# Layer 0's back part: pairs of chunks, or one chunk in each of five parts

## Chip, cores and metric

The kernel runs on one core of one Trainium2 chip. The metric is device microseconds (us) of one execution of the whole program; the median of several executions is given, and one execution is recorded by the hardware profiler.

## What is computed

Two layers on an image of 64 x 64 pixels with 96 channels. Each layer adds a state-space mixer to the image and then a small MLP whose operands are rounded to fp8. Only the end of layer 0's mixer, layer 0's MLP and the first projection of layer 1 matter here:

```
y = _layernorm(y1 + y2 + back(y3) + back(y4), ln_g, ln_b)   # 192 channels
x = x + (y * silu(z)) @ out_proj_w                           # 192 -> 96
t = _ln_t(x)                                                 # per pixel, 96 channels
h = relu(q_acc(q_acc(q_mul(t) @ q_mul(W1).T) + q_mul(b1)))   # 96 -> 384
x = x + q_acc(q_acc(q_mul(h) @ q_mul(W2).T) + q_mul(b2))     # 384 -> 96
xz = _ln_c(x) @ W_in.T                                       # layer 1: 96 -> 192 used here
```

## The kernel before

The 4096 pixels are eight chunks of 512. `back0` (L1019) runs the lines above once for each chunk. The short names used below are those of the tiles:

- **m** (`centred`, L1064): the mean over 192 channels, as 512-column fp32 matmuls with a constant matrix, for a pair of chunks at once, because the upper 64 channels of two chunks share one tile; VectorE subtracts it (L1075, L1076), ScalarE squares (**sq**, L1079), GpSimd multiplies by the gate (L1081).
- **ov** (`variance`, L1083): the variance of the pair by three matmuls (L1088), its root on ScalarE (osd, L1090), a transfer into another layout on the SP queue (or, L1093), a reciprocal on VectorE (L1094).
- **o** (`gated_out`, L1098): the output projection of a chunk, eight matmuls of 128x96 (L596, L597) in one PSUM tile; VectorE scales each quarter by the factor and adds it to the image (L1106). Then `mlp_norm` (L1957): `norm_chunk` (L159: two sums and two scalings on VectorE, a square and a root on ScalarE), rounded to fp8, copied to bf16 by GpSimd (**xb**, L1960).
- **tf** (`mlp_turn`, L1963): four transposes of xb, copied to **xf** by ScalarE (L189).
- **h** (`mlp_up`, L1969): three 512-column matmuls h0, h1, h2 (L1977) from xf, each into one of two PSUM buffers. ScalarE casts each to fp16 (L1979); the bias and relu of h0 run on ScalarE (L1981), those of h1 and h2 on VectorE (L1983); GpSimd casts to fp8 (h8, L1985).
- **of** (`mlp_down`, L1988): twelve matmuls of 128x96 (L1997) that take the three h8 tiles in turn, four times; ScalarE casts (L2002), VectorE adds bias and image (L2003, L2004). Then `norm_chunk` again, giving **lnxnc**.
- **tr** (`to_layer1`, L1109): four fp32 transposes of lnxnc, copied to xt by ScalarE (L189) and stored (L1114).
- **in** (`keep_in_proj`, L1117; `in_proj`, L327): two 512-column fp32 matmuls into layer 1's padded image, copied by ScalarE and VectorE (L333).

The order on TensorE is written out by hand: every matmul goes through `keep` (L1061), which holds it in program order. The order on VectorE, ScalarE and GpSimd is chosen by a scheduler when the program is built; each engine then runs its list in order. PSUM buffers: three for m and in, two shared by ov, o and of, two for h, one shared by tf and tr.

The loop of `back0` goes over four pairs of chunks. For a pair, TensorE's order is m (of this pair, in the step before), o of both chunks, tr and in of the previous pair's two chunks, ov of the next pair, tf of both, h of both, of of both. Layer 1's convolution follows the last in; its first matmul is L1176, then L1209.

Of the kernel before, what the change touches and what calls it, by code (L numbers as in the profile page):

```python
# [28 lines left out]
F32 = mybir.dt.float32  # L29
# [5 lines left out]
ALU = mybir.AluOpType  # L35
# [4 lines left out]
P = 128  # L40
# [3 lines left out]
CD = 96  # L44
# [3 lines left out]
HID = 384  # L48
CH = 512
NCH = L // CH  # L50
# [56 lines left out]
def chunk(c):  # L107
    return slice(c * CH, (c + 1) * CH)
# [12 lines left out]
class Net:  # L121
# [897 lines left out]
    def back0(self):  # L1019

        tc = self.tc
        self.xn_d = self.scratch("xn1", [CD, L])
        with ExitStack() as ctx:
            self.tp = ctx.enter_context(tc.tile_pool(name="af0", bufs=3))
            self.lp = ctx.enter_context(tc.tile_pool(name="al0", bufs=2))
            self.pa = ctx.enter_context(tc.tile_pool(name="ps_a0", bufs=3, space=PSUM))  # L1030
            self.po = ctx.enter_context(tc.tile_pool(name="ps_o0", bufs=2, space=PSUM))
            self.ph = ctx.enter_context(tc.tile_pool(name="ps_h0", bufs=2, space=PSUM))
            self.pt = ctx.enter_context(tc.tile_pool(name="ps_t0", bufs=1, space=PSUM))
            self.w_in = self.w_in1
            n = NCH // 2
            self.sq, self.factor, self.xb, self.xn, self.xt, self.hid = {}, {}, {}, {}, {}, {}

            def chunks(s):
                c0 = s // 2 * 4 + s % 2
                return (c0, c0 + 2) if 0 <= s < n else ()  # L1040

            for s in range(-1, n + 1):
                if s + 1 < n:
                    self.centred(s + 1, chunks(s + 1))
                if 0 <= s < n:
                    self.gated_out(s, chunks(s))
                for c in chunks(s - 1):
                    self.to_layer1(c)
                for c in chunks(s - 1):
                    self.keep_in_proj(c)  # L1050
                if s + 1 < n:
                    self.variance(s + 1, chunks(s + 1))
                for c in chunks(s):
                    self.mlp_turn(0, c)
                for c in chunks(s):
                    self.mlp_up(0, c)
                for c in chunks(s):
                    self.mlp_down(0, c)
                    self.xn[c] = self.norm_chunk(self.lp, c, self.eps6, F32, f"c{c}")

    def keep(self, instruction):  # L1061
        self.tc.keep_in_program_order(instruction)
# [32 lines left out]
        for k, c in enumerate(chunks):  # L1095
            self.factor[c] = r[:, k]

    def gated_out(self, s, chunks):  # L1098

        nc = self.nc  # L1100
        for c in chunks:
            o = self.po.tile([P, 4, CD], F32, tag="o", name=f"o0{c}")
            self.out_proj(o, self.y, self.wg, c, self.keep)
            for j in range(4):
                to, r = self.res[:, c, j, :], self.factor[c][:, j : j + 1]
                nc.vector.scalar_tensor_tensor(to, o[:, j, :], r, to, ALU.mult, ALU.add)  # L1106
            self.mlp_norm(0, c)

    def to_layer1(self, c):  # L1109
        nc = self.nc  # L1110
        xt = self.tp.tile([CD, CH], F32, tag="xt1", name=f"xt1{c}")
        t = self.pt.tile([P, CH], F32, tag="t", name=f"tr1{c}")
        self.to_channels(t, self.xn.pop(c), self.ident, xt, keep=self.keep)
        nc.sync.dma_start(self.xn_d[:, chunk(c)], xt)  # L1114
        self.xt[c] = xt

    def keep_in_proj(self, c):  # L1117
        self.in_proj(self.pa, "a", self.xt.pop(c), self.pad1, c, f"1{c}", self.keep)

# [844 lines left out]
        self.to_channels(t, self.xb.pop(c), self.identb, xt, "c (j p) -> c j p", self.keep)  # L1966
        self.xt[c] = xt

    def mlp_up(self, li, c):  # L1969

        nc = self.nc
        w1, w2, b1, b2 = self.mlp_w[li]
        xt = self.xt.pop(c)
        self.hid[c] = []
        for m in range(HID // P):
            a = self.ph.tile([P, CH], F32, tag="h", name=f"h{li}{c}{m}")
            self.keep(nc.tensor.matmul(a, w1[:, m * P : (m + 1) * P], xt, start=True, stop=True))  # L1977
            h16 = self.tp.tile([P, CH], F16, tag="h16", name=f"h16{li}{c}{m}")
            nc.scalar.copy(h16, a)  # L1979
            if m == 0:  # L1980
                nc.scalar.activation(h16, h16, AF.Relu, bias=b1[:, m : m + 1])  # L1981
            else:
                nc.vector.tensor_scalar(h16, h16, b1[:, m : m + 1], 0.0, ALU.add, ALU.max)  # L1983
            h8 = self.tp.tile([P, CH], FP8, tag=f"h8{m}", name=f"h8{li}{c}{m}")
            nc.gpsimd.tensor_copy(h8, h16, saturate=False)  # L1985
            self.hid[c].append(h8)
# [100 lines left out]
```

## Time and profile before

| quantity | us |
|---|---|
| median of 11 runs (1486.65 to 1496.18) | 1487.85 |
| profiled execution | 1487.29 |
| its span, first to last instruction | 1485.5 |
| the back of layer 0: first m to layer 1's first matmul | 120.74 to 280.71 |
| TensorE busy from 119 to 281 | 128.19 |
| VectorE, ScalarE, GpSimd busy there | 75.32, 59.55, 35.27 |

How to read the views: the page divides the span into 40 slices and gives a digit for the busy tenths of each engine, and for the clock granted to TensorE. Busy time can be asked for any stretch of the span. The waits say which instruction of which engine ended the idle time of an engine, with total, number and longest. The timeline lists instructions with start and duration in us, and in brackets the idle time before. PE is TensorE, DVE VectorE, ACT ScalarE, POOL GpSimd, SP the queue of the transfers. A fp32 matmul shows as two records.

### The profile page before, as it was taken

The numbers are of one execution on the slowest core, as the hardware profiler recorded it, in microseconds if no ns is written. First come the engines' busy times: TensorE is split into PE (matmuls) and PEld (weight loads), VectorE is DVE, ScalarE is ACT, GpSimd is POOL, SyncE is SP. The second block draws the span as 40 slices with busy tenths as digits, with TensorE's granted clock in tenths as the row PEclk, the third lists the DMA queues.
The fourth block names the chain that finished last, engine by engine and source line by source line (L and its number), as shares of the span: only waits on it lengthen the run. The fifth ranks groups of instructions, "written<-read, shape, count | busy, mean of one in ns | idle before, by whom it ended". The sixth has DMA issues, their size and how long they took to land. (4 is left out here: it accounts for less than half of the span.)

```text
span 1485.5 us, 13012 instructions
## 1 busy us (share of the span) xinstructions
PE 1182.8 (80%) x4040; PEld 493.9 (33%) x4040; DVE 1155.5 (78%) x887; ACT 907.5 (61%) x1091; POOL 785.2 (53%) x461
## 2 busy tenths in 40 slices
PE   7998887799995477667777677687777888899875
PEld 4533444343331122222222222222222343344343
DVE  6593445203337999999999999999999999999875
ACT  4463333204446677677777777777777777787434
POOL 1002221100001787778777877777778777875545
PEclk9998666799997688888888888988888898987955
DMA  2242000013217745635555454645364557342201
GB/s 63 63 138 56 11 11 12 11 29 85 78 49 216 224 137 178 239 115 159 181 172 182 135 183 159 189 128 187 121 227 130 179 161 252 123 148 71 87 0 43
DMA packets 68851, 183.21 MB, mean 123 GB/s; under 512 B 21488, under 2 KB 35460, under 8 KB 61956
## 3 DMA queue, kind: packets, MB, share of 16 engines
q1 hardware_dynamic: 67480, 182.00, 39.8%
q8 instruction: 34, 0.56, 0.2%
q10 hardware_dynamic: 1292, 0.28, 0.1%
q14 instruction: 45, 0.37, 0.1%
HBM read 155.98 MB, written 20.47 MB: 119 GB/s over the span
## 5 line engine op out<-in xcount | busy, mean ns | idle before, releaser
L1552 POOL TENSOR_TENSOR hss<-h1s,xws 128x1024 f32<-128x1024 f32 x96 | 224.6, 2377 | 132.3 <-PE hs L1560 132.3
L1536 ACT ACTIVATE da<-dt1s,a 128x1024 f32<-128x1024 f32 x168 | 187.8, 1118 | 149.0 <-DVE xws L1547 87.8
L1560 PE MATMUL hs<-hss,ident 128*128 128x512 f32 x376 | 212.0, 647 | 58.9 <-DMA x2s<-bc 32.9
L1547 DVE TENSOR_TENSOR_SCAN xws<-da,xws 128x1024 f32<-128x1024 f32 x96 | 224.1, 2335 | 10.4 <-DVE xws L1547 2.7
L1536 ACT ACTIVATE da<-dt0s,a 128x1024 f32<-128x1024 f32 x168 | 187.0, 1113 | 69.3 <-DVE xws L1547 52.2
L1560 PE MATMUL hs<-h0s,ident 128*128 128x512 f32 x376 | 199.3, 612 | 0.4 <-DVE h0s L1547 0.4
L1547 DVE TENSOR_TENSOR_SCAN h1s<-da,h1s,xws 128x1024 f32<-128x1024 f32 x72 | 169.2, 2350 | 10.4 <-ACT da L1536 1.3
L1560 PEld LDWEIGHTS hs<-hss,ident 128*128 128x128 f32 x376 | 68.6, 200 | 193.2 <-issue 78.4
L1375 POOL TENSOR_TENSOR dun<-u,dtn 128x512 f32<-128x512 f32 x4 | 5.9, 1482 | 197.8 <-DVE dtn L1272 107.6
L1560 PEld LDWEIGHTS hs<-h0s,ident 128*128 128x128 f32 x376 | 74.2, 198 | 97.7 <-issue 92.5
L1581 PE MATMUL acc<-hc2s,fold 128*32 128x512 f32 x128 | 47.1, 825 | 61.0 <-POOL hc2s L1570 57.9
L1581 PE MATMUL acc<-hc0s,fold 128*32 128x512 f32 x128 | 46.3, 813 | 53.4 <-POOL hc0s L1570 53.4
L1581 PE MATMUL acc<-hc1s,fold 128*32 128x512 f32 x128 | 46.5, 816 | 50.1 <-POOL hc1s L1570 50.1
L1520 POOL TENSOR_TENSOR x1s<-x1s,dus 128x1024 f32<-128x1024 f32 x32 | 75.1, 2368 | 8.9 <-DMA x1s<-bc 8.9
L1520 POOL TENSOR_TENSOR x2s<-x2s,dus 128x1024 f32<-128x1024 f32 x32 | 75.1, 2362 | 6.6 <-DMA c1s<-bc 6.6
L1547 DVE TENSOR_TENSOR_SCAN x0s<-da,x0s 128x1024 f32<-128x1024 f32 x32 | 74.7, 2335 | 4.3 <-ACT da L1536 1.9
L1547 DVE TENSOR_TENSOR_SCAN x1s<-da,x1s 128x1024 f32<-128x1024 f32 x32 | 74.7, 2335 | 3.5 <-ACT da L1536 0.9
L1547 DVE TENSOR_TENSOR_SCAN x2s<-da,x2s 128x1024 f32<-128x1024 f32 x32 | 74.7, 2335 | 3.4 <-ACT da L1536 0.8
L1560 PE MATMUL hs<-x0s,ident 128*128 128x512 f32 x128 | 66.9, 604 | 0.2 <-DVE x0s L1547 0.2
L1560 PE MATMUL hs<-x1s,ident 128*128 128x512 f32 x128 | 66.6, 602 | 0.0
L1520 POOL TENSOR_TENSOR x0s<-x0s,dus 128x1024 f32<-128x1024 f32 x28 | 65.7, 2361 | 0.0
L1232 PE MATMUL cv<-pad,cw 128*128 128x512 f32 x144 | 64.3, 598 | 0.0
(343 smaller groups left out, 2415.8 us busy)
## 6 DMA issues: line engine op xcount, KB each, us to landing
c0s<-bc SPq DMA_DIRECT2D x184, 128.0 KB, 2.6
c1s<-bc SPq DMA_DIRECT2D x184, 128.0 KB, 2.6
x2s<-bc SPq DMA_DIRECT2D x32, 512.0 KB, 5.0
x0s<-bc SPq DMA_DIRECT2D x28, 512.0 KB, 3.5
x1s<-bc SPq DMA_DIRECT2D x28, 512.0 KB, 6.0
dus<-du SPq DMA_DIRECT2D x20, 512.0 KB, 7.0
dt1s<-dt SPq DMA_DIRECT2D x40, 256.0 KB, 6.5
dt0s<-dt SPq DMA_DIRECT2D x40, 256.0 KB, 4.8
```

The lines of the kernel that those rows point to most:

```text
L1232: keep(nc.tensor.matmul(t, cw[0][:, tap, 0:P], v, start=tap == 0, stop=False))
L1375: keep(nc.gpsimd.tensor_tensor(dun, u[1][:, m], dtn, ALU.mult))
L1520: keep(nc.gpsimd.tensor_tensor(x, x, du[:, part[j]], ALU.mult))
L1536: keep(nc.scalar.activation(das[i, s], dts[o][:, part[j]], AF.Exp, scale=self.a6[:, g, k : k + 1]))
L1547: keep(nc.vector.tensor_tensor_scan(to, da, x, start, ALU.mult, ALU.add))
L1552: keep(nc.gpsimd.tensor_tensor(cols(hs)[:, w, :], grid(h1)[:, w, :], grid(xw)[:, w, :], ALU.add))
L1560: keep(nc.tensor.matmul(t, self.ident, x[:, chunk(m)], start=x is hs, stop=x is xs[i % 3]))
L1581: keep(nc.tensor.matmul(to, self.fold4, src, start=k == 0, stop=k == NK - 1))
```

## The change

The loop goes over twelve steps. In step t, of goes to chunk t-3 of the sequence, in to chunk t-4, m or ov (in turn) to the pair t // 2, o to chunk t-1, tf and h to chunk t-2, and tr to chunk t-3, between the second and third h. The order inside a step is as written. `gated_out` takes one chunk, `mlp_up` takes the list of the blocks to do, the norms' pool has three buffers for each tile, and layer 1's turned chunks have their own dictionary.

```diff
-            self.lp = ctx.enter_context(tc.tile_pool(name="al0", bufs=2))
+            self.lp = ctx.enter_context(tc.tile_pool(name="al0", bufs=3))
...
             def chunks(s):
                 c0 = s // 2 * 4 + s % 2
-                return (c0, c0 + 2) if 0 <= s < n else ()
-
-            for s in range(-1, n + 1):
-                if s + 1 < n:
-                    self.centred(s + 1, chunks(s + 1))
-                if 0 <= s < n:
-                    self.gated_out(s, chunks(s))
-                for c in chunks(s - 1):
-                    self.to_layer1(c)
-                for c in chunks(s - 1):
-                    self.keep_in_proj(c)
-                if s + 1 < n:
-                    self.variance(s + 1, chunks(s + 1))
-                for c in chunks(s):
-                    self.mlp_turn(0, c)
-                for c in chunks(s):
-                    self.mlp_up(0, c)
-                for c in chunks(s):
-                    self.mlp_down(0, c)
-                    self.xn[c] = self.norm_chunk(self.lp, c, self.eps6, F32, f"c{c}")
+                return (c0, c0 + 2)
+
+            def chunk_of(q):
+                return chunks(q // 2)[q % 2] if 0 <= q < NCH else None
+
+            for t in range(NCH + 4):
+                s = t // 2
+                out, up, down, last = (chunk_of(t - d) for d in (1, 2, 3, 4))
+                if down is not None:
+                    self.mlp_down(0, down)
+                    self.xn[down] = self.norm_chunk(self.lp, down, self.eps6, F32, f"c{down}")
+                if last is not None:
+                    self.keep_in_proj(last)
+                if s < n:
+                    (self.variance if t % 2 else self.centred)(s, chunks(s))
+                if out is not None:
+                    self.gated_out(out)
+                if up is not None:
+                    self.mlp_turn(0, up)
+                    self.mlp_up(0, up, (0, 1))
+                if down is not None:
+                    self.to_layer1(down)
+                if up is not None:
+                    self.mlp_up(0, up, (2,))
...
-    def gated_out(self, s, chunks):
+    def gated_out(self, c):
...
-        for c in chunks:
-            o = self.po.tile([P, 4, CD], F32, tag="o", name=f"o0{c}")
-            self.out_proj(o, self.y, self.wg, c, self.keep)
-            for j in range(4):
-                to, r = self.res[:, c, j, :], self.factor[c][:, j : j + 1]
-                nc.vector.scalar_tensor_tensor(to, o[:, j, :], r, to, ALU.mult, ALU.add)
-            self.mlp_norm(0, c)
+        o = self.po.tile([P, 4, CD], F32, tag="o", name=f"o0{c}")
+        self.out_proj(o, self.y, self.wg, c, self.keep)
+        for j in range(4):
+            to, r = self.res[:, c, j, :], self.factor[c][:, j : j + 1]
+            nc.vector.scalar_tensor_tensor(to, o[:, j, :], r, to, ALU.mult, ALU.add)
+        self.mlp_norm(0, c)
...
-    def mlp_up(self, li, c):
+    def mlp_up(self, li, c, parts):
...
-        for m in range(HID // P):
+        for m in parts:
```

More of the change, by code (lines that the diff above doesn't have):

```diff
@@ L1035, in back0 @@
             n = NCH // 2
-            self.sq, self.factor, self.xb, self.xn, self.xt, self.hid = {}, {}, {}, {}, {}, {}
+            self.sq, self.factor, self.xb, self.xn, self.xt, self.xt1, self.hid = {}, {}, {}, {}, {}, {}, {}
             def chunks(s):
                 c0 = s // 2 * 4 + s % 2
-                return (c0, c0 + 2) if 0 <= s < n else ()
-            for s in range(-1, n + 1):
-                if s + 1 < n:
-                    self.centred(s + 1, chunks(s + 1))
-                if 0 <= s < n:
-                    self.gated_out(s, chunks(s))
-                for c in chunks(s - 1):
-                    self.to_layer1(c)
-                for c in chunks(s - 1):
-                    self.keep_in_proj(c)
-                if s + 1 < n:
-                    self.variance(s + 1, chunks(s + 1))
-                for c in chunks(s):
-                    self.mlp_turn(0, c)
-                for c in chunks(s):
-                    self.mlp_up(0, c)
-                for c in chunks(s):
-                    self.mlp_down(0, c)
-                    self.xn[c] = self.norm_chunk(self.lp, c, self.eps6, F32, f"c{c}")
+                return (c0, c0 + 2)
[20 more added lines that the diff above has]
+                    self.mlp_up(0, up, (2,))
     def keep(self, instruction):
@@ L1114, in to_layer1 @@
         nc.sync.dma_start(self.xn_d[:, chunk(c)], xt)
-        self.xt[c] = xt
+        self.xt1[c] = xt
     def keep_in_proj(self, c):
-        self.in_proj(self.pa, "a", self.xt.pop(c), self.pad1, c, f"1{c}", self.keep)
+        self.in_proj(self.pa, "a", self.xt1.pop(c), self.pad1, c, f"1{c}", self.keep)
     def layer1(self, w, pool):
@@ L1967, in mlp_turn @@
         self.xt[c] = xt
-    def mlp_up(self, li, c):
+    def mlp_up(self, li, c, parts):
         nc = self.nc
         w1, w2, b1, b2 = self.mlp_w[li]
-        xt = self.xt.pop(c)
-        self.hid[c] = []
-        for m in range(HID // P):
+        xt = self.xt[c]
+        self.hid.setdefault(c, [])
+        for m in parts:
             a = self.ph.tile([P, CH], F32, tag="h", name=f"h{li}{c}{m}")
```

## The prediction

> **What bounds the kernel now.** First the page. The changed code runs in slices 4 to 8 of 40 (37.1 us each), and there the tensor engine is the fullest engine, but it has gaps (the digits give the busy tenths of each slice):
>
> ```profile
> PE   7998887799995477667777677687777888899875
> ```
>
> The busy time by stretches cuts this out. Columns: length, busy time of PE, weight loads, DVE, ACT, POOL, then granted clock. The stretches are pair 1, pair 2, pair 3 without the next pair's mean, the drain, and the whole stage from its first matmul to layer 1's first.
>
> ```profile
> 160.50:198.40 37.90, 31.69 (x103) 17.07 (x101) 18.69 (x44) 14.12 (x28) 8.74 (x11) 0.68 0.04 11
> 198.40:236.40 38.00, 31.56 (x103) 17.09 (x101) 18.69 (x44) 14.12 (x28) 8.73 (x11) 0.68 0.04 11
> 236.40:267.00 30.60, 24.07 (x90) 15.06 (x88) 16.30 (x39) 11.76 (x24) 4.77 (x8) 0.61 0.06 14
> 267.00:281.00 14.00, 8.07 (x19) 3.79 (x18) 6.20 (x13) 4.46 (x9) 0.00 (x0) 0.59 0.10 28
> 119.00:281.00 162.00, 128.19 (x402) 68.15 (x402) 75.32 (x172) 59.55 (x114) 35.27 (x48) 0.67 0.09 23
> ```
>
> PE sets the pace; about 34 us of 162 are PE waits. Who ends them, from the waits of PE in this stage:
>
> ```profile
> PE tf L188 <- POOL xb L1960: 10.3, 5, 3.1
> PE tr L188 <- DVE lnxnc L180: 6.2, 2, 4.4
> PE of L1997 <- POOL h L1985: 5.6, 8, 0.7
> PE h L1977 <- ACT h L1979: 5.0, 8, 0.7
> ```
>
> The first two (16.5 us) are norm chains PE reaches too early. The last two (10.6) are the hidden layer's chain: PE h, ACT cast, DVE relu, POOL cast, PE of. In the timeline of pair 1 (start, length) its end reads:
>
> ```profile
> 190.46 0.42 PE L188 MATMUL tf<-identb,xb 128*96 128x128 bf16 x4 [2.55 <-POOL xb L1960]
> ...
> 195.39 0.58 ACT L1979 CAST h<-h 128x512 f16<-128x512 f32 x1
> ...
> 196.00 0.71 DVE L1983 TENSOR_SCALAR h<-h,b 128x512 f16<-128x512 f16 x1 [0.74 <-ACT h L1979]
> ...
> 196.84 0.81 POOL L1985 CAST h<-h 128x512 fp8e5<-128x512 f16 x1 [0.28 <-DVE h L1983]
> ...
> 197.70 0.98 PE L1997 MATMUL of<-w2q,h 128*128 128x96 fp8e5 x10 [0.74 <-POOL h L1985]
> ```
>
> From the end of the second tf (190.88) to the last relu'd block's use (197.70) are 6.8 us, paid once per **two** chunks. Last, the clock, in stretches I set to its own steps: the transitions lie 3.41 us apart or multiples of it.
>
> ```profile
> 135.11:138.52 3.41, 3.41 (x12) 2.94 (x11) 1.12 (x4) 1.12 (x2) 3.10 (x3) 1.00 0.00 0
> 138.52:141.93 3.41, 3.41 (x11) 2.60 (x10) 0.56 (x3) 0.00 (x0) 0.00 (x0) 0.50 0.01 2
> 145.35:148.76 3.41, 3.41 (x5) 0.31 (x3) 2.37 (x7) 0.70 (x2) 0.50 (x1) 0.50 0.00 0
> 148.76:152.17 3.41, 0.49 (x5) 0.28 (x4) 1.29 (x3) 1.86 (x4) 0.36 (x1) 1.00 0.04 1
> ```
>
> The output projection (128x96, all of 135.11 to 138.52) fills PE, yet the clock then halves; 512-column fp32 matmuls (m, ov, in) for about 2.9 us of a stretch or more bring it back, 1.85 us do not (159.0 to 162.4). I use this as the rule of this trace.
>
> **The change, part by part.** Nothing is removed or added in arithmetic: the same matmuls, evictions and eight `or` transfers. What moves is PE's hand-written order. A step now runs: of(c), in(c'), then m of a pair (even steps) or ov (odd steps), o(c''), tf, h0, h1, tr, h2 - and the next step opens with of of the very chunk whose h2 was just issued.
>
> Prices: fp32 512-column record 0.92 us at clock 0.50 and 0.44 at 1.00 (in: 8 records in 5.09 us from 251.59, 2.9 of it slow: 3.2 + 4.8 records). o of a chunk 5.1 to 5.7 (8 x 0.64 or 0.71). tf 0.4, tr 1.1, of's last ten matmuls 1.0.
>
> *Gone:* tf's wait (10.3): xb is now made a step earlier; its chain (o's end to tf about 5.1 us, 143.7 to 148.8) lies under the next step's of, in, m or ov and o (over 12 us); without that cover it costs 5.1 a step. h's wait (5.0) for its PSUM buffer: tr's 1.1 us stands there. Part of the drain: in of chunk 5 lies beside the last norm.
>
> *New 1: tf to h.* Between tf and h0 PE has nothing: ACT copies xf (0.58 and two hops), 0.75 us each step.
>
> *New 2: h2 to of.* Behind of stand in, m/ov and o, all of PE. The **tail** from tf's end to of's third matmul, on ACT's queue with the rows' lengths: odd step: xf to 0.69, cast h0 to 1.8, cast h1 to 2.35, relu h0 to 3.0, copy xt to 3.55, cast h2 to 4.1, then DVE 0.6, POOL 0.7 and hops: **5.75**. Even step: two squares of the pair (0.63 each) and lnsqb stand between: **6.65**. PE works 2.75 of each (three h, tr, two of), so it idles 3.0 or 3.9.
>
> *New 3: tr* needs lnxnc, made by DVE and ACT behind the in copies: hidden under o in steps 3 to 7. In step 8 (no m) DVE holds o's first eviction ahead of that norm's second sum, in step 9 (no o) ACT holds its square behind cast h0 and its root behind cast h1: tr starts 2.2 and 3.4 us after h1, and the tails are 7.7 and 8.8 (each piece again at its row's length).
>
> *Costed at nothing:* the third norm buffer (al0 2 to 3), DVE (75.3 busy of 162) and POOL (35.3); or's transfer (issue 188.30 to reciprocal 190.96, 2.7 us) lies under o (5.2 us), else it costs up to 2.7 an odd step. On SP one xn store per step stands ahead of the next or, its data ready before.
>
> Ledger, in us on the profile's clock (a step t counts from of's third matmul). A run of in with m or ov goes slowly until the first boundary (155.58, 159.0, 162.4 and so on) that ends a stretch it filled for 2.5 us or more. t4: 172.65 to 176.06 slow, 3.7 records, the other 8.3 at 0.44 take 3.65, in all 7.05. t6 starts 2.1 us ahead of a boundary and must go on to the next: 6 records slow in 5.5, 6 fast in 2.65.
> - t0 to t2: same to 130.0; o 135.6, m 138.7, o 144.2. tf waits for xb 5.1 us here, since ov no longer fills it: 149.7; tail without tr 5.4: 155.1 (of is already running, which the old order reached at 156.7).
> - t3: of 1.0 + ov 4.15 + o 5.25 + tf 0.4 + 5.75 = 16.55 to 171.65.
> - t4: 1.0 + in and m 7.05 + 5.3 + 0.4 + 6.65: 192.05. t5: 1.0 + in and ov 6.2 + 5.1 + 0.4 + 5.75: 210.5.
> - t6: 1.0 + 8.15 + 5.2 + 0.4 + 6.65: 231.9. t7: 1.0 + 6.8 + 5.1 + 0.4 + 5.75: 250.95.
> - t8: 1.0 + in 3.1 + o 5.2 + 0.4 + 7.7: 268.35. t9: 1.0 + in 3.7 + 0.4 + 8.8: 282.25.
> - drain: of 1.0, in 3.7, its copy 0.7 ahead of the norm on DVE, norm 3.1, tr 1.0, xt 0.75, in 3.65, copy 0.8: 296.95.
>
> Layer 1's first matmul was at 280.71: **+16.2 us**. So a pair t4+t5 is 38.85 against 37.9, t6+t7 40.45; the rest is fill and drain, where waits two chunks once shared are now paid by each. The profiled execution took 1487.29 (span 1485.5): 1503.5, I say 1503; the median 1487.85 differs by 0.6, which I leave.
>
> Bounds: tails are not in the old trace; below, PE's own work in one (2.75), above, the old two-chunk tail 6.8 and 2 us of misplaced queue. Dense runs: 9.2 us a pair at full clock, 19.3 at half; I take 13 to 15, nearest to the 13.4 of the old pair, as a run must cross one slow stretch.
>
> A rule on the clock speaks the other way. The Trainium skill ("TensorE: Matmul & The Clock Gate", section "Why this matters for your kernels") says that gaps under about 3 us keep the clock full. The trace differs: the clock halved at 138.5 after PE had been 3.41 of 3.41 us busy. By the rule all dense runs would be fast (17 us less, about 1486).
>
> **Rivals.**
> 1. *The tail is hidden, faster.* Were h8 ready when PE has issued h2, steps 3 to 9 lose 3.0+3.9+3.0+3.9+3.0+4.95+6.05 = 27.8 us: 1475.5. For it: waits of 16.5 us do go. Against: nothing stands between h2 and of on PE, and ACT's five pieces before cast h2 alone take 3 us. Deciding point: a mean wait ahead of of and h0 under 1.7 us a step rather than 4.0.
> 2. *A wash.* Tails 1 us shorter (7 us), and five dense runs meet a clock boundary one stretch sooner (1.78 each, 8.9): 1487.
> 3. *The clock stays half* through dense runs: 12 or 10 records at 0.92, some 14.5 us more: 1518. Against: a run of over 7 us always holds a whole slow stretch.
> 4. That one chunk per step is not what happens is excluded: PE's order is kept by hand, and it holds one chunk of each part per step.
>
> **How the numbers follow.** Forecast 0.81 (1492 to 1512), hidden tail 0.06, wash 0.07 (of it 0.02 faster), half clock 0.06. Within 0.2% is about what a measurement can tell from no change. Faster 0.08, same 0.05, slower 0.87. The range takes the forecast with tails 1 us off either way and clock boundaries one stretch off: 1491 to 1512.
>
> **What would show it.** Right: PE waits of "of <- POOL h" near 2 to 3 us each in steps 3 to 9 (some 20 in sum, from 5.6), h behind ACT xf near 0.75 eight times, one tf wait near 5 at the start and no other; layer 1's first matmul near 297. Wrong: of waits under 1 us, PE's share of the stage above 0.85, a granted clock in it well above 0.67, or that matmul before 281.

## The result and the profile after

| kernel | median us | lowest to highest | runs |
|---|---|---|---|
| before | 1490.15 | 1484.97 to 1502.38 | 50 |
| after | 1505.91 | 1500.34 to 1516.61 | 13 |

The changed kernel is slower: its time is 1.0111 times that of before, 95% interval 1.0091 to 1.0131, which is 16.5 us with 3 us either way. (The 50 runs of before include the 11 of the table ahead of the change.) The forecast was 1503 in a range from 1491 to 1512.

The profiled execution took 1506.15 us with a span of 1504.3, 18.8 more than the span of before. Three parts make it up. (1) The first m starts at 126.36 instead of 120.74, **5.6 us** later, in code ahead of the back that the change does not touch. (2) From there to layer 1's first matmul are 170.7 us instead of 160.0, **10.7 us** more. (3) The convolution that follows, from that first matmul to the first 64-row matmul of its second part (L1237, in after L1241), takes 41.4 instead of 39.5, **1.9 us** more; the remaining 0.6 us I did not place.

The page's row for PE, in 40 slices of 37.6 us:

```profile
PE   7998788599999177767877777777777888899975
```

The eighth digit (263 to 301 us), the end of the stage, is 5 where the page of before has 7; there layer 1 filled PE from 280.71 on.

The busy times by stretches say where the 10.7 us are. I cut both traces at the same events: the back's start, for each pair the start of the last ten "of" matmuls of its second chunk, and layer 1's first matmul. Columns as in the prediction: length, then busy PE, weight loads, DVE, ACT, POOL, then granted clock. Before, the fill, the first full pair and the last pair:

```profile
120.74:159.78 39.04, 32.08 (x89) 14.42 (x89) 14.76 (x34) 15.09 (x25) 13.03 (x18) 0.73 0.23 51
159.78:197.70 37.92, 31.72 (x100) 17.09 (x101) 18.71 (x44) 14.12 (x28) 8.74 (x11) 0.68 0.04 11
...
235.72:266.04 30.32, 23.79 (x86) 14.97 (x87) 16.04 (x39) 11.76 (x24) 4.77 (x8) 0.61 0.06 14
```

After, at the same events:

```profile
126.36:176.66 50.30, 38.61 (x109) 19.69 (x109) 18.73 (x45) 16.91 (x29) 13.09 (x18) 0.74 0.19 44
176.66:215.37 38.71, 32.57 (x100) 17.76 (x101) 18.73 (x43) 13.89 (x29) 9.04 (x11) 0.68 0.04 10
...
253.29:282.53 29.24, 18.81 (x71) 11.54 (x71) 13.95 (x32) 10.85 (x24) 5.76 (x8) 0.62 0.05 14
```

All five lengths, with those of the last experiment but one (kept2, told below):

| stretch, us | before | after | kept2 |
|---|---|---|---|
| fill, to pair 0's second "of" | 39.0 | 50.3 | 51.7 |
| to pair 1's | 37.9 | 38.7 | 30.6 |
| to pair 2's | 38.0 | 37.9 | 28.6 |
| to pair 3's | 30.3 | 29.2 | 29.7 |
| drain, to layer 1 | 14.7 | 14.5 | 12.9 |

The two full pairs cost the same (+0.8 and -0.1). The fill costs 11.3 more: 6.5 us of PE's work that the new order already has behind it at that event (chunk 2's o among it), and 4.7 us more idle PE. In the last pair PE has 5.0 us less to do, yet the pair is only 1.1 shorter: waits fill the place of the work that was brought forward. So the pipeline borrows in the fill and is not paid back at the end. Over the whole back, PE is idle for 7.6 us more (39.6 instead of 32.1), and the same matmuls keep it busy for 3.2 us more (131.06 instead of 127.90): about 70% of the loss is waiting, the rest slower matmuls.

That the full pairs cost the same does not mean that nothing changed in them. Over both, PE waited 12.3 us before: tf for xb 5.4, of for h8 2.8, h for ACT 2.8, tr for ACT 1.3. After, the waits of PE in the same two pairs (total, times, longest) are 13.5:

```profile
PE of L2001 <- POOL h L1989: 10.8, 11, 1.7
PE h L1981 <- ACT xf L189: 2.7, 4, 0.7
```

Over the whole back, the waits that answer to those shown in the prediction:

```profile
PE of L2001 <- POOL h L1989: 17.5, 16, 2.2
PE tr L188 <- DVE lnxnc L180: 8.8, 3, 3.6
PE h L1981 <- ACT xf L189: 5.4, 8, 0.7
PE tf L188 <- POOL xb L1964: 4.3, 1, 4.3
```

The new wait is the tail of the hidden layer. The timeline of the end of step 4 (start, duration, idle before) shows it row by row; tf to the last use of h8 is one chain over four engines:

```profile
189.44 0.66 PE L188 MATMUL tf<-identb,xb 128*96 128x128 bf16 x4
190.14 0.58 ACT L189 COPY xf<-tf 96x512 bf16<-96x512 bf16 x1 [4.47 <-PE tf L188]
...
192.43 0.63 PE L1981 MATMUL h<-xf,w 96*128 96x512 bf16 x1
...
193.54 0.58 ACT L189 COPY xt<-tr 96x512 f32<-96x512 f32 x1
...
194.02 0.53 ACT L175 ACTIVATE lnsqb<-lnxcb 128x384 f32<-128x384 f32 x1
...
194.44 0.58 ACT L1983 CAST h<-h 128x512 f16<-128x512 f32 x1
...
195.47 0.61 POOL L1989 CAST h<-h 128x512 fp8e5<-128x512 f16 x1 [0.22 <-DVE h L1987]
196.14 0.98 PE L2001 MATMUL of<-w2q,h 128*128 128x96 fp8e5 x10 [0.57 <-POOL h L1989]
```

PE has issued h2 at 192.43, and its cast on ACT starts only at 194.44, behind a relu and a cast (192.46 and 193.07), the xt copy and the norm's square; of's last ten start 6.0 us after the end of tf (190.10).

### The profile page after: what moved, and what is told of

The parts are those of the page before. It is cut to its first block, busy times and chain, and to the rows that moved or that the text cites. A ratio compares the mean times of both kernels' runs of the same rounds, so it can differ in the third digit from the quotient of the medians.

```text
span 1504.3 us, 13016 instructions
## 1 busy us (share of the span) xinstructions
PE 1197.6 (80%) x4040; PEld 500.7 (33%) x4040; DVE 1155.6 (77%) x887; ACT 905.9 (60%) x1091; POOL 786.8 (52%) x461
## 3 DMA queue, kind: packets, MB, share of 16 engines
q1 hardware_dynamic: 67480, 182.00, 39.4%
## 5 line engine op out<-in xcount | busy, mean ns | idle before, releaser
L1551 DVE TENSOR_TENSOR_SCAN h1s<-da,h1s,xws 128x1024 f32<-128x1024 f32 x72 | 169.2, 2350 | 12.6 <-DVE h1s L1551 2.9
```

The lines of the kernel that those rows point to most:

```text
L1551: keep(nc.vector.tensor_tensor_scan(to, da, x, start, ALU.mult, ALU.add))
```

## The experiments

The theory: the tail stands open because "of" is the next matmul behind h2, so every chunk pays it. The rivals: the third norm buffer or the scheduler's order on ACT and DVE makes the loss (so the place of "of" is not what counts), or the TensorE clock does.

**How much of this is the program and how much is the run.** Both kernels again, unchanged (each ratio in this section is to the kernel before, with its 95% interval):

> The kernel before, unchanged, profiled a second time. Theory (the stage itself got longer by its waits, the front's time only varies): layer 0's back takes 160 us again (158 to 162), while the start of the back moves by up to 6 us from run to run. Rival (the back varies as much as the front): the back differs from 160 by more than 3 us.

> The changed kernel, unchanged, profiled a second time. Theory: the back takes 170.7 us again (168 to 174, the clock's boundaries fall differently), and the time from layer 1's first matmul on is some 2 us longer than before because that layer starts at the half clock. Rival (most of the difference is the front's luck of the first profile, 5.6 us): the back comes out within 3 us of the 160 of before.

Before again: 1495.53 us, ratio 1.0027 (0.9996 to 1.0058); its back took 160.0 us. After again: 1505.04 us, ratio 1.0112 (1.0042 to 1.0182); back 170.3, the convolution part 41.4, span 1498.5. The first m was now at 120.9, as in before, so the 5.6 us of part (1) are not in every execution of after. That they are only luck is not shown: the first m came at 120.9 to 130.5 us in the ten profiles of after and its variants, and at 119.9 to 123.6 in the three of before and its variant. Between two profiles with equal fronts the difference is 1498.5 - 1485.5 = 13.0 us, and the back holds 10.3 of them. Ten runs of the unchanged kernel before came out at 1.0027, so ratios of about 1.003 below cannot be told from before by the time; there the argument goes by the stretches and waits of the profile.

**The third norm buffer (al2).**

```diff
-            self.lp = ctx.enter_context(tc.tile_pool(name="al0", bufs=3))
+            self.lp = ctx.enter_context(tc.tile_pool(name="al0", bufs=2))
```

> The changed kernel with two buffers in the norms' pool instead of three: one small part of the change undone. Theory (the wait of the second MLP product for its third block is what costs): no difference, back 170.7 us within 2, median within 3 us of the changed kernel. Rival (the pool's buffers matter): new waits behind the norms, back over 174 us.

Time 1503.61, ratio 1.0088 (1.0047 to 1.0129): the interval covers nearly all of after's, so two buffers do not mend the loss, and the median is within the 3 us expected. The profile missed the expectation: its back took 176.7 us, over the 174 that the rival named, but without the rival's new waits behind the norms. The waits had hardly changed (of 16.9 us, tr 9.3), but PE was busy longer with the same matmuls, at a lower granted clock:

```profile
130.40:307.10 176.70, 137.32 (x400) 71.36 (x401) 76.58 (x172) 58.56 (x114) 36.41 (x48) 0.64 0.09 21
```

After's PE was busy for 131.06 us at 0.67 in its back. So 6.3 us of PE time hang on where the clock's stretches fall on the steps. The first m of al2 was at 130.4, and the medians agree, so I take this as the execution's luck and not the buffer's doing. The runs speak for it: six of al2's ten took 1498.8 to 1504.0 us and four 1513.2 to 1515.0, the profiled one (1514.66) among the four, and after has such runs too (up to 1516.6 us). One profile of al2 cannot prove it.

**The tail alone, in the old order (pair_serial).** In the kernel before, each chunk's MLP runs to its end before the next one's:

```diff
                 for c in chunks(s):
                     self.mlp_turn(0, c)
-                for c in chunks(s):
                     self.mlp_up(0, c)
-                for c in chunks(s):
                     self.mlp_down(0, c)
```

> The kernel before, with its pairs, but the MLP of a pair done chunk after chunk (tf, h, of, then tf, h, of of the other) instead of both tf, both h, both of: the one part of the change that I hold to cost most, alone. Theory (the chain from tf to the last use of h is then paid by each chunk): 2 x (0.4 + 5.4 + 1.0) = 13.6 us a pair instead of 11.0, so the back grows by some 10 us to 167 to 173, with the waits of the second product for its blocks near 18 us instead of 5.6 and the wait of tf for xb smaller than 10.3. Rival (the clock or the drain makes the loss): the back stays within 3 us of 160.

The back took 166.1 us, 6.1 more than before and a little under what was expected; time 1499.19, ratio 1.0032 (0.9994 to 1.0069). The tf wait is gone, h waits 7.4 us for xf, and "of" waits:

```profile
PE of L1995 <- POOL h L1983: 17.4, 20, 1.7
```

Of the change this kernel has only that tf, h and "of" of one chunk run in one piece, so that "of" follows its own h2. The wait of "of" goes from 5.6 to 17.4 us, near after's 17.5. This isolates the tail as the price of not sharing it between two chunks, and clears the pipeline's other parts of that one wait. It lengthens the back by 6.1 of the 10.7 us; in the time of the whole program the loss is not clear of noise.

**The second projection later in the step (of_late).** "of" and its norm are put behind in and m or ov:

```diff
-                if down is not None:
-                    self.mlp_down(0, down)
-                    self.xn[down] = self.norm_chunk(self.lp, down, self.eps6, F32, f"c{down}")
                 if last is not None:
                     self.keep_in_proj(last)
                 if s < n:
                     (self.variance if t % 2 else self.centred)(s, chunks(s))
+                if down is not None:
+                    self.mlp_down(0, down)
+                    self.xn[down] = self.norm_chunk(self.lp, down, self.eps6, F32, f"c{down}")
```

> The changed kernel with the second MLP product (and the norm after it) moved behind in and m or ov of its step, nothing else moved. Theory (it waits because it directly follows the last h on TensorE): its waits fall from 17.5 us to under 3; but the norm behind it starts some 6 us later while the transpose that needs it stays, and I expect 1.5 to 2.5 us of new wait there in each of eight steps; back 159 to 167 us. Rival (the clock, not the wait, makes the stage long): waits may move, the back stays at 169 us or more.

Missed: 1509.19, ratio 1.0112 (1.0049 to 1.0175), back 177.7. The wait of "of" is gone, as meant, and another came in its place:

```profile
PE tr L188 <- DVE lnxnc L180: 29.6, 8, 5.3
```

The timeline of one step of of_late shows who delays lnxnc:

```profile
188.19 0.32 DVE L1110 SCALAR_TENSOR_TENSOR res<-o,or,res 128x96 f32<-128x96 f32 x1 [2.46 <-PE o L597]
188.42 0.55 DVE L2008 TENSOR_TENSOR res<-res,o 128x384 f32<-128x384 f32 x1
...
189.11 0.54 DVE L171 TENSOR_REDUCE lnmc<-res 128x4 f32<-128x384 f32 x1
...
194.24 1.06 PE L188 MATMUL tr<-ident,lnxnc 128*96 128x128 f32 x4 [3.82 <-DVE lnxnc L180]
```

DVE had nothing to do for 2.46 us. The next instruction in its list, the first eviction of o (L1110), waits for all of o, and L2008, whose operand L2007 had made by 185.7, stands behind it. The list's order was chosen by the scheduler. So the order on the other engines does count, as that rival says, but here as what eats the gain.

**tf earlier (tf_early).** tf is put ahead of o:

```diff
+                if up is not None:
+                    self.mlp_turn(0, up)
                 if out is not None:
                     self.gated_out(out)
                 if up is not None:
-                    self.mlp_turn(0, up)
                     self.mlp_up(0, up, (0, 1))
```

> The changed kernel with tf one place earlier, ahead of the output projection. Theory: h's waits for xf (5.4 us) go, the tail of h to of stays on TensorE but without xf and the pair's squares on ScalarE, so of's waits fall from 17.5 to some 14; back 160 to 166 us. Rival (these waits are covered by others): back 169 us or more.

Missed: 1509.61, ratio 1.0108 (1.007 to 1.0147), back 170.4. The wait of h for xf fell from 5.4 to 0.7 us as meant, and tf's own wait rose by the same 5.3, from 4.3 to 9.6, of which 7.7 in step 2, where xb is not yet made. That of "of" stayed at 16.7.

**The clock in the drain (warm_drain).** Two 512-column fp32 matmuls whose results nobody reads follow in of chunk 5 in the drain:

```diff
+                if t == NCH + 2:
+                    warm = self.pa.tile([P, CH], F32, tag="a", name="warm1")
+                    for i in range(2):
+                        self.keep(self.nc.tensor.matmul(warm, self.mean, self.y[0][:, chunk(i)], start=True, stop=True))
```

> The changed kernel with two more fp32 matmuls of 512 columns, whose result nobody reads, after in of chunk 5 in the drain, where TensorE waits 3.6 us for the last norm. Theory (the drain's single in calls do not fill a stretch of the clock, so the last in and layer 1's first matmuls run at half): the last in falls from 3.8 to about 2 us and the 41.4 us from layer 1's first matmul to its first wide 64-row one fall to 39.5; some 3.8 us less in all, with the waits as they were. Rival (work added on TensorE costs): no gain or a loss of up to 3.7 us.

Met: 1499.88, ratio 1.0038 (1.0002 to 1.0073). The back took 168.1 us and the convolution part 39.4, together 4.6 less than in after. The last in of after's drain:

```profile
292.40 3.78 PE L331 MATMUL in<-xt,w_in 96*128 96x512 f32 x4 [0.67 <-ACT xt L189]
```

and of warm_drain's:

```profile
290.11 1.98 PE L331 MATMUL in<-xt,w_in 96*128 96x512 f32 x4 [0.67 <-ACT xt L189]
```

The last in takes 1.98 us instead of 3.78, and layer 1 starts at full clock. That settles part (3): after's drain spends its 14.5 us at clock 0.50, and layer 1's convolution pays for it until 301.2.

**Something to do in the tail (fill_wait).** One such unread matmul stands between h2 and the next of in steps 3 to 9:

```diff
+                if 3 <= t < NCH + 2:
+                    warm = self.pa.tile([P, CH], F32, tag="a", name=f"warm{t}")
+                    self.keep(self.nc.tensor.matmul(warm, self.mean, self.y[0][:, chunk(0)], start=True, stop=True))
```

> The changed kernel with one more fp32 matmul of 512 columns, whose result nobody reads, between the last h of a step and the second MLP product of the next, in steps 3 to 9: TensorE's wait there is filled with work that counts for the clock. Theory (the wait is the loss, the clock comes second): of's waits fall by about 1.8 us a step to some 5 in sum but nothing is won by that itself; the runs of in with m or ov start 1.8 us nearer to the clock's rise, 1 us a step; back 161 to 169 us. Rival (the half clock is the whole loss): back 158 us or less.

Met: 1496.69, ratio 1.0031 (0.9995 to 1.0066), back 165.9. PE does more and the back is 4.8 us shorter than after's:

```profile
126.10:292.00 165.90, 137.01 (x414) 72.70 (x415) 75.87 (x172) 58.55 (x114) 36.95 (x48) 0.71 0.09 22
```

The wait of "of" shows 6.8 us, since the unread matmuls lie in it. What is gained is clock, 0.71 instead of 0.67: the seven unread matmuls show 12.9 us, yet PE's busy time rose by only 6.0, so the others ran faster in sum. A part of what the open tail costs is thus slower matmuls behind it, and not the wait itself.

**Order on all engines by hand (kept).** On PE: in, m or ov, of, tf, o, h0, h1, tr, h2. The norms, the evictions of o and of, the casts on ScalarE and the copies of xf and xt are held in program order too, and xb's norm is issued last:

```diff
         m, v, r = small("lnm"), small("lnv"), small("lnr")
-        nc.vector.tensor_reduce(m, x, AX.X, ALU.add)
+        keep(nc.vector.tensor_reduce(m, x, AX.X, ALU.add))
...
-        nc.scalar.copy(to, t[0:CD])
+        keep(nc.scalar.copy(to, t[0:CD]))
...
+                    self.xn[down] = self.norm_chunk(self.lp, down, self.eps6, F32, f"c{down}", self.keep)
+                if up is not None:
+                    self.mlp_turn(0, up)
                 if out is not None:
                     self.gated_out(out)
...
                     self.mlp_up(0, up, (2,))
+                if out is not None:
+                    self.mlp_norm(0, out)
```

> The changed pipeline with another order: in, m or ov, of and its norm, tf, o, h0, h1, tr, h2; the norm behind of and the copies of the hidden layer are held in this order on VectorE and ScalarE too, so that the output projection's eviction does not stand ahead of that norm, and the norm behind o comes after the hidden layer. Theory (three waits make the loss: of behind h2, h behind xf, tr behind the norm): of's and h's waits under 2 us each, tr's under 10 (the drain's three stay), back 148 to 156 us, total 1477 to 1485, under both kernels. Rival (the half clock sets the back): waits fall, but TensorE's busy time grows by as much and the back stays over 160.

Missed: 1505.02, ratio 1.0105 (1.0061 to 1.015), back 169.2. "of" waits for nothing any more, but h waits 15.0 us for xf. One step:

```profile
181.54 0.39 PE L188 MATMUL tf<-identb,xb 128*96 128x128 bf16 x4
188.22 0.52 ACT L175 ACTIVATE lnsqc<-lnxcc 128x384 f32<-128x384 f32 x1 [3.48 <-DVE lnxcc L173]
...
189.57 0.56 ACT L189 COPY xf<-tf 96x512 bf16<-96x512 bf16 x1
...
190.18 1.01 PE L1983 MATMUL h<-xf,w 96*128 96x512 bf16 x2 [3.17 <-ACT xf L189]
```

tf is done at 181.93, and its copy runs at 189.57, because I had written the norm ahead of it: ACT idles 3.48 us for the norm's first operand with the ready copy behind it. This is the same fault as in of_late, made by hand.

**The order mended (kept2).** m or ov, in, of, tf, then of's norm, o, h0, h1, tr, h2, xb's norm (in step 2, where xb is young, tf stays behind o):

```diff
-                if down is not None:
-                    self.mlp_down(0, down)
-                    self.xn[down] = self.norm_chunk(self.lp, down, self.eps6, F32, f"c{down}")
-                if last is not None:
-                    self.keep_in_proj(last)
                 if s < n:
                     (self.variance if t % 2 else self.centred)(s, chunks(s))
+                if last is not None:
+                    self.keep_in_proj(last)
+                if down is not None:
+                    self.mlp_down(0, down)
+                if up is not None and t > 2:
+                    self.mlp_turn(0, up)
+                if down is not None:
+                    self.xn[down] = self.norm_chunk(self.lp, down, self.eps6, F32, f"c{down}", self.keep)
                 if out is not None:
                     self.gated_out(out)
+                if up is not None and t == 2:
+                    self.mlp_turn(0, up)
                 if up is not None:
-                    self.mlp_turn(0, up)
                     self.mlp_up(0, up, (0, 1))
...
+                if out is not None:
+                    self.mlp_norm(0, out)
```

> The order held on three engines, second try: m or ov, in, of, tf, then of's norm (behind xf on ScalarE), o, h0, h1, tr, h2, and last the norm behind o; in step 2 tf stays behind o. Theory (the first try lost to xf queued behind the norm's root, 15.0 us, and to in directly behind its own transpose, 5.8 us; both are moved): of and h wait under 3 us each in sum, tf under 7, tr under 8, in under 1; back 145 to 154 us, median 1473 to 1482, under both kernels. Rival (TensorE's own work at the half clock is the floor): waits fall to some 20 us, but busy time rises and the back stays over 156.

1483.58 us, ratio 0.9958 (0.9927 to 0.999): 22 us under after and 0.4% under before, which its interval only just tells from no change; the median lies just above the range expected. The back took 153.5 us, within the range. "of" waits for nothing and h for 1.5 us, as expected, but tf (10.5 us, expected under 7), tr (9.3, under 8) and in (3.1, under 1) wait longer. Its stretches stand in the table above (cut at the start of all twelve "of" matmuls, since none of them waits). The first full pair:

```profile
173.73:204.31 30.58, 29.38 (x102) 15.74 (x100) 19.36 (x43) 13.86 (x28) 8.31 (x11) 0.78 0.05 13
```

The fill is about as long as after's. The full pairs fall from 38 to 30.6 and 28.6 us, with PE busy for 29.4 of 30.6 at clock 0.78: where the gaps go, the clock goes up too. In the last two stretches the norms' latency is bare again (tf waits 2.9 us twice, tr 5.3 once), and the granted clock is 0.50 throughout.

**kept2 with the drain's two unread matmuls (kept2w).** The edit is warm_drain's, put behind "of".

> The second try with the two unread matmuls in the drain that kept the clock up before. Theory: the last in and layer 1's first matmuls run at the full clock, 2 to 4 us less than the second try, back and layer 1's start taken together. Rival: the drain's in calls now lie elsewhere against the clock and nothing is won.

1484.46, ratio 0.9969 (0.9933 to 1.0005), back 153.9: no gain over kept2. The last in still took 3.78 us. The two matmuls did raise the clock, but too early: it was full from 270.1 to 273.5. PE then stood idle for 2.6 us until the last norm was done, and the last in began only at 275.44, at 0.50 again. Their row in kept2w:

```profile
268.21 2.87 PE L1058 MATMUL warm<-y,mean 128*128 128x512 f32 x4
```

## Why the prediction came out right, point by point

The sign and the mechanism held. The back was put too large (16.2 us forecast, 10.7 and 10.3 measured), and that the total came out near all the same is in part luck: layer 1's cold start (1.9 us), which the ledger did not hold, made up for a part, in the first profile the late front (5.6 us) for the rest, and of the 15.8 us between the medians some 3 lie in neither the back nor layer 1 and stay unplaced.

- **The tail (New 2)** is right. "of" waited 17.5 us over the steps against "some 20"; from the end of tf's row to "of"'s third matmul, odd tails took 5.6 (forecast 5.75), even ones 6.0 and 6.1 (6.65), step 8's 7.5 (7.7), step 9's 7.8 (8.8). pair_serial shows the cause without the rest of the change. The even tails were half a us shorter because the first of the pair's squares (190.62 to 191.25) ran while ACT would have waited for h0 anyway.
- **tf to h (New 1)** is right: 0.67 us eight times, against 0.75.
- **tf's wait** is right: one, of 4.3 us, in the fill (forecast about 5), the others gone.
- **tr (New 3)** is right: 2.0 us in step 8 and 3.2 in step 9 (2.2 and 3.4 forecast), and 3.6 in the drain.
- **The ledger's sizes** are what was off, by 5.5 us in the back. Over steps 3 to 9, the runs of in, m and ov were put 1.8 us too long in sum, the tails with tf 1.6, and "of" 1.4 (it took 0.78 us a step in place of 1.0). The largest single miss is the clock's phase in step 6, 19.0 us long and not 21.4: the forecast let its run of in and m cross a second slow stretch (8.15 us). In the trace, in started at 216.15, 3.1 us ahead of a boundary instead of 2.1, the clock rose there, and the run took 6.2. Some 0.6 of that is price: m's last four records took 1.13 us at full clock, where the ledger has 0.44 each. Step 9 took 12.06 for 13.9 (the tail 1.0 and in 0.6 us shorter), step 4 0.9 less, but step 5 0.8 more. al2's back, 176.7, shows how far such phases can move it: the sum put one phase of the clock where only a range of some 6 us could be known.
- **Layer 1's cold start** was not in the ledger, which ended at layer 1's first matmul: +1.9 us, shown by warm_drain.
- **The front** moved by 5.6 us in the first profile. "Layer 1's first matmul near 297" was met at 297.06, but only by this: without it, it would have been 291.4, and in after_again it was 291.18.
- **Rival 1 (the tail is hidden)** fell: its waits, which the forecast put at 27.8 us over steps 3 to 9 with those of tr in steps 8 and 9, were 17.5 + 5.4 + 2.0 + 3.2, less 2.7 for step 2's own tail, or 25.4: 3.6 us a step against 4.0, or 2.9 without those of tr, and 1.7 was the deciding point. (Its time, 1503.5 less 27.8, is 1475.7, not 1475.5.) Rival 2 needed 15.9 us less than the ledger, and 5.5 came. Rival 3 is excluded by the runs of in with m or ov themselves, 6.2 to 7.1 us in steps 4 to 7, where it has 12 or 10 records at 0.92, so 11.0 or 9.2 us.

On the rule of the Trainium skill that I set against the trace ("TensorE: Matmul & The Clock Gate", "Why this matters for your kernels": against drops in mid-kernel it asks for no idle gaps over about 3 us between bursts of matmuls), the result decides as the trace of before did: between 176.66 and 253.29 no wait of PE was longer than 1.7 us, and the granted clock there was 0.68.

What stays open: the medians differ by 15.8 us (of 13 and 50 runs) and the two like profiles by 13.0. The front and the clock's phase move single executions by more than that difference, and I have not separated them.

## What to carry to other kernels

When a pair is split into single steps, look at what the in-order engine issues right behind the last producer: if the consumer of that chain is next, each step pays the chain's whole latency, and here the pipeline became a small gain only with independent work in between and the other engines' order set to match (kept2). Moving a matmul alone is half of the change, because the in-order lists of the other engines then decide: a ready instruction that stands behind a waiting one (L2008 in of_late, the xf copy in kept) gives the wait back under another name. Count the fill and the drain of the pipeline by themselves: here the fill took 11 to 13 us more in both orders (with 6.5 and 11.1 us more of PE's work behind it), so with only four pairs the steady state has to win that back first.

## What the runs showed of the hardware

- The time for which the clock is down early on is worth as much as the change does to the back. The unchanged code ahead of the first m took 119.9 to 130.5 us over the profiles; in before the clock was down from 19 to 22.5 us of the span, in after from 18 to 35. With the clock down equally long, the kernels agree: down for 3.4 us, the first m came at 120.7 in before and 120.9 in after_again; for 10.2 us, at 123.6 in both pair_serial (a variant of before) and kept (of after). With 27.3 us down, it came at 130.4 and 130.5 in al2 and tf_early. The Trainium skill ("TensorE: Matmul & The Clock Gate", "What's actually happening") says that the window runs freely at 3413 ns and that the cold part varies from run to run. The 3.41 us grid of these traces agrees. It also rates the ramp under 1% of a typical span: the front's spread of 10.6 us is 0.7% of 1485, so that holds too, but the effect to be measured here is of the same size, 1.1%.
- More work took less time: the seven unread matmuls of fill_wait added 6.0 us to PE's busy time and made the back 4.8 us shorter.
- What raises the clock is not the time of the 512-column matmuls alone. In after, 2.7 us of in (from 254.07) raised it at 256.76, and 2.6 us (from 271.25) at 273.84, with the matmuls of "of" filling nearly all the rest of the stretch; 3.0 us of in (chunk 5, until 287.06) did not raise it at 287.48, and there PE stood idle for the last 0.4 us. So the prediction's "2.5 us or more" held in this trace where PE was busy for the rest of the stretch. The three stretches (length, busy PE and so on, the clock 0.50 in each):

```profile
253.35:256.76 3.41, 3.41 (x14) 1.86 (x15) 2.49 (x6) 1.26 (x3) 0.17 (x1) 0.50 0.00 0
270.43:273.84 3.41, 3.37 (x13) 1.92 (x14) 1.67 (x3) 0.99 (x2) 0.43 (x1) 0.50 0.02 5
284.07:287.48 3.41, 2.98 (x4) 0.67 (x2) 2.04 (x4) 0.59 (x1) 0.00 (x0) 0.50 0.09 3
```
